# Background work of an attention and FFN kernel in fixed places, one operation at a time

## The chip, the cores and the metric

The kernel runs on one core of a Trainium2 chip. The metric is the time on the device in microseconds (us), lower is better. The core has five engines that run their own instruction queues side by side: PE (TensorE, matrix products; its weight loads are shown apart as PEld), DVE (VectorE), ACT (ScalarE), POOL (GpSimd) and SP (SyncE, which here only issues DMA transfers). Each queue is worked off in order: an instruction that waits holds up everything behind it on its engine.

## What is computed

One transformer block in float32: 16 sequences of 256 tokens, width 256, 16 heads of 128, causal attention, then an FFN with 2048 hidden units whose weights are 4-bit codes with a scale for each 32 values.

```python
def block(x):
    q, k, v = (einsum('bpd,hde->bphe', ln(x), W) + b for W, b in (Q, K, V))
    scores = einsum('bqhe,bkhe->bhqk', q, k) / sqrt(128)
    attn = softmax(where(causal, scores, -1e5))
    z = einsum('bkhe,bhqk->bqhe', v, attn)
    x = x + ln(einsum('bqhe,hed->bqd', z, W_O) + b_O)
    Wg, Wu, Wd = dequant(gate), dequant(up), dequant(down)   # LUT[code] * scale
    h = gelu_tanh(ln(x) @ Wg.T) * (ln(x) @ Wu.T)
    return x + ln(h @ Wd.T)
```

`ln` is a layer norm over the last axis without gain and bias.

## The kernel before

**Tiling.** The 4096 tokens are 8 blocks of 512 (two sequences each). A value that goes into a matrix product is split into a high and a low part (float32r), and three products (high-high, low-high, high-low) make one. In attention a *unit* is one head of one block: `units` lists block b, group g, head j of the group (L375), N = 128 in all; two units are a *pair*, which shares one load of weights. The FFN works on 4 superblocks of 1024 tokens with 8 groups of 256 hidden units each; its gate and up products go by a scheme with seven products in place of eight (class `Two`), for which `x_ops` makes sums and differences of the activations.

**The loop over units** (L941 to L985) is a software pipeline. Iteration i starts the scores and the softmax of unit i+3 (`st_s`), computes K and Q of unit i+4 (`st_qk`), turns the softmax of unit i+3 (`st_t`, a DVE transpose into `tr`), adds to the attention output (`st_o`), multiplies probabilities and values of unit i (`st_z`), splits the probabilities of unit i+1 (`st_p`: `ph` on ACT, `pl` on POOL), computes a part of V (`st_v`), loads the turned probabilities of unit i+2 (`st_b`: `pt` from `hop`) and stores those of unit i+3 (`st_w`: four transfers from `tr` to `hop`). The softmax of a unit goes: `sc` on PE; mask and row minimum `mn` on DVE; exponential `pr` and its sum on ACT; reciprocal `rc` on DVE; scaling of `pr` on POOL; `tr` on DVE; `hop`; `pt`.

**The order is written by hand.** `run` (L98) puts every instruction behind the last one of its engine in program order, and `dma` (L86) does the same for all transfers, which all go out on SP. So the place at which the program issues an operation is its place in its engine's queue.

**Weights.** In the first block, `w_split` splits each weight as it is first used (high part on ACT; low part on DVE for K and Q, on POOL for V and O), and a later `w_keep` writes it back to DRAM. From then on `w_get` (L345) loads the split weights: `wk` and `wq` of pair p+3 at the end of an even iteration, `wo` of pair p+1 and half of `wv` at the end of an odd one (L977), 512 KB each. There are two buffers for each weight.

**Background.** All that isn't the pipeline itself stands in generators, in four queues: `urgent` (`ln1`, the layer norm of the next block's tokens; the FFN's `end`), `splits` (weights of the first block), `behind` (`mid`: attention output back to token order, layer norm, residual, second layer norm, hop into the FFN's order; and `end`) and `idle` (`f_make` for 24 pieces of FFN weights, then `x_ops`). A `yield` ends a step; its number says how many slots to wait, a negative one that the queue goes on to its next step at once if that is due. `slot` (L140) advances a clock, writes what is overdue (`late`), and lets each of the four queues take a step, as long as an account of estimated columns for DVE and POOL (`credit`, `share`, `spent`) isn't overdrawn; `slot(True)` stops after the first. One step can hold several operations on several engines: in `f_make`, three DVE operations in a row (L623 to L625), or four POOL operations, or an ACT copy with a POOL operation behind it (L652).

Slots stand at three places of an iteration: `slot(True)` inside `st_s`, between the first and the second reciprocal and scaling (L463), and two calls behind `st_qk` (L959, L960). The loop over FFN groups has five (L1009 to L1021).

What is needed and not there yet is forced: `await_`, `f_get` (loads of FFN weights) and `Two.product` run steps of a queue until it is there.

Of the kernel before, what the change touches and what calls it, by code (L numbers as in the profile page):

```python
# [28 lines left out]
def kernel(  # L29
# [65 lines left out]

    spent = [0, 0]

    def run(op, dst, *args, **kw):  # L98
        if op.__self__ in (nc.vector, nc.gpsimd):
            cols = max(math.prod(ap.shape[1:]) for ap in (dst, args[0]))  # L100
            if op == nc.vector.tensor_scalar:
                cols //= 2
            spent[op.__self__ is nc.gpsimd] += 100 + cols
        with ExitStack() as behind:
            for m in last.values():
                behind.enter_context(tc.issue_after(m))
            ins = op(dst, *args, **kw)  # L107
        last[ins.ins.engine] = ins.ins
        return ins
# [3 lines left out]
    urgent, behind, splits, idle = deque(), deque(), deque(), deque()  # L113
# [3 lines left out]
    def step(jobs, force=False):  # L117
        while jobs and (force or jobs[0][1] <= now[0]):
            try:
                wait = next(jobs[0][0]) or 1  # L120
            except StopIteration:
                jobs.popleft()
                continue
            jobs[0][1] = now[0] + abs(wait)
            if wait > 0:
                return True
        return False

    def add(jobs, job):
        jobs.append([job, 0])  # L130
# [6 lines left out]
    share = [480, 560]  # L137
    credit = [0, 0]

    def slot(one=False):  # L140
# [3 lines left out]
        for e in range(2):  # L144
            credit[e] = min(credit[e] + share[e], 4 * share[e])
        for jobs in (urgent, splits, behind, idle):
            before = list(spent)
            if (jobs is splits or min(credit) > 0) and step(jobs):
                if jobs is not splits:
                    for e in range(2):  # L150
                        credit[e] -= spent[e] - before[e]
                    if one:
                        return

    def finish(jobs):
        while jobs:
            step(jobs, True)
            overdue(now[0] + 2)

    def await_(found, key, jobs):  # L160
        while key not in found:
            step(jobs, True)
# [6 lines left out]
    def ln_stats(srcs):  # L169
# [5 lines left out]
        for t in range(n):  # L175
            run(nc.vector.bn_stats, st[:, t, :], srcs[t])
            if t % 2:
                yield
        for t in range(n):
            run(nc.vector.bn_aggr, mv[:, t, :], st[:, t, :])  # L180
        run(nc.vector.tensor_scalar, rs[:, :n], mv[:, :n, 1], EPS, None, ALU.add)
        run(nc.gpsimd.tensor_tensor, rs[:, :n], rs[:, :n], mhalf[:, :n], ALU.pow)
        yield
# [5 lines left out]
    def ln_apply(dst, src, mv, rs, t):  # L189
        spent[1] += D  # L190
# [28 lines left out]
    def turn_tokens(hop, xn):  # L219
        tr = wide("xtr").rearrange("p a b -> p (a b)").rearrange("p (k m i) -> p k m i", k=4, m=8)  # L220
        for kt in range(2):
# [5 lines left out]
            yield 1 + kt  # L227
        spread(hop, tr.rearrange("p k m i -> p k (m i)"))
        yield -3

    def split_tokens(key, hop):
        xr = wide("xr")
        dma(xr, hop)
        yield -5
        xr = xr.rearrange("p a (m i) -> p m a i", m=8)
        xt = work.tile([P, 2, 2, TB], F32R, tag="xT", name="xT", bufs=4)
        for kt in range(2):
# [4 lines left out]
            yield  # L242
# [3 lines left out]
    def ln1(b):  # L246
        xs = [x_load(x, b, hf) for hf in range(2)]
        yield -4
        mv, rs = yield from ln_stats([xs[hf][:, t, :] for hf in range(2) for t in range(2)])
        xn = wide("xn")  # L250
        for t in range(4):
            ln_apply(xn[:, t, :], xs[t // 2][:, t % 2, :], mv, rs, t)
            yield
        hop = dram.tile([P, 4, 2 * P], F32, tag="xhop", name="xhop", bufs=2)
        yield from turn_tokens(hop, xn)
        yield from split_tokens((1, b), hop)

    def first_tokens():

        xs = [x_load(x, 0, hf) for hf in range(2)]  # L260
        yield
# [49 lines left out]
    def w_split(p, n):  # L311
# [21 lines left out]
        if done:  # L333
            W[key, n] = w_view(w)
            late.append((now[0] + 2, w_keep, (key, n, w)))
# [5 lines left out]
    def split(p, n):  # L341
        w_split(p, n)
        yield

    def w_get(p, n):  # L345

        if p < NG:
            add(splits, split(p, n))
        elif p < len(pairs):
            overdue(now[0] + 2)  # L350
# [82 lines left out]
    def st_s(u):  # L433
# [22 lines left out]
        for bi in range(2):  # L456
# [5 lines left out]
            if bi:  # L462
                slot(True)  # L463
# [55 lines left out]
    def st_o(p, dh):  # L519
# [13 lines left out]
        if g == NG - 1:  # L533
# [3 lines left out]
            if dh == 1:  # L537
                add(behind, mid(b, PO.pop(b)))
# [11 lines left out]
    def back_load(tr):  # L550
# [3 lines left out]
        yield -3  # L554
        o = wide("o")
        dma(o, hop)
        yield -5
# [8 lines left out]
    def mid(b, oT):  # L566

        tr = back_tile()
        for dh in range(2):
            back(tr, dh, oT[:, dh])  # L570
            yield 1 + dh
        o = yield from back_load(tr)
        xs = [x_load(x, b, hf) for hf in range(2)]
        xt = [xs[t // 2][:, t % 2, :] for t in range(4)]
        mv, rs = yield from ln_stats(o)
        att = wide("att")
        for t in range(4):
            ln_apply(cols4(att[:, t, :]), o[t], mv, rs, t)
            yield
        for hf in range(2):  # L580
            run(nc.gpsimd.tensor_tensor, xs[hf], xs[hf], att[:, 2 * hf : 2 * hf + 2, :], ALU.add)
            yield
# [4 lines left out]
        for t in range(4):  # L587
            ln_apply(pairs_of_h(xn[:, t, :], True), pairs_of_h(xt[t], False), mv, rs, t)
            yield
# [18 lines left out]
    def f_make(g, n, then):  # L608
# [4 lines left out]
        def small_tile(dtype, name):  # L613
            return work.tile([P, 2, 256], dtype, tag="code", name=name, bufs=3)
# [5 lines left out]
        yield  # L620
        if then:
            f_load(*then)
        run(nc.vector.tensor_scalar, sg, c, 8.0, -2.0, ALU.is_ge, ALU.mult)  # L623
        run(nc.vector.tensor_scalar, c, c, 7, None, ALU.bitwise_and)
        run(nc.vector.tensor_scalar, t, c, 2.0, 8.0, ALU.mult, ALU.subtract)  # L625
        yield
        run(nc.vector.scalar_tensor_tensor, v, c, 0.5, t, ALU.mult, ALU.max)
        run(nc.vector.scalar_tensor_tensor, v, c, 2.0, v, ALU.subtract, ALU.max)
        yield
        run(nc.vector.scalar_tensor_tensor, v, sg, 1.0, v, ALU.add, ALU.mult)  # L630
        scb = sc.unsqueeze(1).to_broadcast([P, 2, 256])
        if n == "d":
# [3 lines left out]
            yield  # L636
            run(nc.scalar.copy, w[:, 0], full)
            run(nc.gpsimd.tensor_tensor, w[:, 1], full, f(w[:, 0]), ALU.subtract)
        else:
# [3 lines left out]
            yield  # L643
# [6 lines left out]
            yield  # L650
            w = f_tile("u")
            run(nc.scalar.copy, w[:, 0], full)  # L652
            run(nc.gpsimd.tensor_tensor, w[:, 1, 0:4], full[:, 0:4], f(w[:, 0, 0:4]), ALU.subtract)
            yield
            run(nc.gpsimd.tensor_tensor, w[:, 1, 4:8], full[:, 4:8], f(w[:, 0, 4:8]), ALU.subtract)
        late.append((now[0] + 2, f_keep, (g, n, w)))
        yield
# [12 lines left out]
    def f_get(k, n):  # L670

        sb, g = divmod(k, NG)
        if sb < NSB:
            while (g, n) not in FD:
                step(idle, True)
# [398 lines left out]
```

## Time and profile before

| | |
|---|---|
| Median of 3 runs | 1589.2 us (1588.15 to 1591.8) |
| The profiled execution, its own time | 1585.9 us |
| its span, first to last instruction | 1584.0 us |
| PE busy in the span | 1524.1 us (96%) |
| DVE, ACT, POOL busy | 1182.3, 1021.6, 789.9 us |
| DMA | 407.55 MB, 257 GB/s on average |
| First score matmul of a unit, first and last of the steady part | 74.52 and 1051.27 us |
| First FFN matmul (`pa`) | 1062.63 us |

The span has three stages: attention up to about 1051 us, a passage of some 30 us in which the last units end while the first FFN products run, and the FFN from there, with a tail of 24 us. Times in the profile are counted from the span's first instruction. A busy PE isn't a PE at its peak, since the end of a matmul is modelled and the next one overlaps it: matmuls of 512 columns are shown with 389 ns, and follow each other every 227 ns. So a late start shows as idle time only where it is longer than that overlap, and the distance between the same matmul of two units is the safer measure. In a line of the timeline, what stands in brackets at the end is the idle time of the engine ahead of the instruction and what ended it; `x4` merges four instructions. SPq is SP's queue of DMA issues: the time of such a line is that of the issue, not of the transfer.

### The profile page before, as it was taken

The numbers are of one execution on the slowest core, as the hardware profiler recorded it, in microseconds if no ns is written. First come the engines' busy times: TensorE is split into PE (matmuls) and PEld (weight loads), VectorE is DVE, ScalarE is ACT, GpSimd is POOL, SyncE is SP. The second block draws the span as 40 slices with busy tenths as digits, with TensorE's granted clock in tenths as the row PEclk, the third lists the DMA queues.
The fourth block names the chain that finished last, engine by engine and source line by source line (L and its number), as shares of the span: only waits on it lengthen the run. The fifth ranks groups of instructions, "written<-read, shape, count | busy, mean of one in ns | idle before, by whom it ended". The sixth has DMA issues, their size and how long they took to land.

```text
span 1584.0 us, 25656 instructions
## 1 busy us (share of the span) xinstructions
PE 1524.1 (96%) x7792; PEld 1277.6 (81%) x7792; DVE 1182.3 (75%) x2944; ACT 1021.6 (64%) x2584; POOL 789.9 (50%) x1017
## 2 busy tenths in 40 slices
PE   8999999999899999999999999989999999999996
PEld 6788788888788878878888888877878778778885
DVE  6776777877777777787778787656877777777865
ACT  6786666666666666666666656656565755666663
POOL 3654668668666665765775774670520410420200
PEclk9999999999999999999999999989999999999998
DMA  8897898998889889889898988876566656645551
GB/s 287 286 328 249 271 325 273 314 300 281 283 259 314 282 275 305 265 283 318 259 297 260 303 284 275 275 223 240 194 239 207 232 194 208 237 185 205 222 210 41
DMA packets 200410, 407.55 MB, mean 257 GB/s; under 512 B 21456, under 2 KB 128464, under 8 KB 189520
## 3 DMA queue, kind: packets, MB, share of 16 engines
q1 hardware_dynamic: 200272, 405.91, 77.2%
q8 instruction: 62, 1.02, 0.3%
q14 instruction: 76, 0.62, 0.1%
HBM read 294.15 MB, written 111.67 MB: 256 GB/s over the span
## 4 chain that ended last, share of the span: by engine, by line
PE 46%; DVE 16%; DMA 13%; ACT 10%; POOL 7%; issue 4%; SPq 4%; DVEq 0%; POOLq 0%; ACTq 0%
PE pd L107 10%; PE pa L107 6%; PE pq L107 4%; PE po L107 4%; SPq L91 4%; PE pk L107 4%; PE pf L107 4%; PE pv L107 4%; PE pz L107 4%; PE sc L107 3%; DVE sum L107 3%; DVE tr L107 3%; ACT pr L107 3%; DMA wq<-wq 3%; DMA wk<-wk 2%
## 5 line engine op out<-in xcount | busy, mean ns | idle before, releaser
L107 ACT ACTIVATE pr<-sc,mn 128x128 f32<-128x128 f32 (+1 forms) x512 | 208.3, 420 | 225.8 <-DVE mn L107 209.2
L107 POOL TENSOR_SCALAR pr<-pr,rc 128x128 f32<-128x128 f32 (+1 forms) x512 | 220.0, 444 | 222.2 <-DVE rc L107 211.7
L107 POOL TENSOR_TENSOR rs<-rs,mhalf 128x4 f32<-128x4 f32 (+1 forms) x33 | 35.8, 1084 | 379.6 <-DVE rs L107 374.0
L107 POOL TENSOR_TENSOR pl<-pt,ph 128x512 fp32r<-128x512 f32 x128 | 168.9, 1320 | 94.2 <-ACT ph L107 94.1
L107 PE MATMUL pk<-xT,wk 128*128 128x512 f32 x768 | 200.4, 396 | 12.8 <-DMA wk<-wk 11.1
L107 PE MATMUL pv<-wv,xT 128*128 128x512 f32 x768 | 209.2, 407 | 1.1 <-DVE vl L107 1.1
L107 PE MATMUL pd<-inter,wd 128*128 128x512 f32 x768 | 199.6, 394 | 4.7 <-ACT inter L107 3.1
L107 PE MATMUL pq<-xT,wq 128*128 128x512 f32 x768 | 197.5, 392 | 4.5 <-DMA wq<-wq 3.3
L107 DVE CUSTOM_DVE_ANT_0 sc<-sc,mask 128x128 f32<-128x128 f32 (+1 forms) x512 | 179.9, 372 | 22.2 <-PE sc L107 12.6
L107 PEld LDWEIGHTS pd<-inter,wd 128*128 128x128 f32 x768 | 143.6, 189 | 40.6 <-ACT inter L107 6.4
L107 PEld LDWEIGHTS pq<-xT,wq 128*128 128x128 f32 x768 | 142.8, 188 | 41.2 <-PE pk L107 6.8
L107 PEld LDWEIGHTS pk<-xT,wk 128*128 128x128 f32 x768 | 134.9, 188 | 38.9 <-DMA wk<-wk 14.4
L107 DVE SCALAR_TENSOR_TENSOR kl<-pk,bqk,kh 128x512 fp32r<-128x512 f32 x128 | 95.9, 750 | 93.4 <-ACT kr L107 93.2
L107 ACT COPY part<-pa 128x512 f32<-128x512 f32 x192 | 111.7, 586 | 76.9 <-PE pa L107 74.4
L107 PE MATMUL po<-zh,wo 128*128 128x512 f32 x512 | 158.7, 391 | 0.0
L107 PEld LDWEIGHTS pv<-wv,xT 128*128 128x128 f32 x768 | 135.0, 189 | 25.5 <-DVE vl L107 2.1
L107 ACT CAST inter<-sum 128x512 fp32r<-128x512 f32 x128 | 80.1, 626 | 99.2 <-DVE sum L107 99.0
L107 DVE STREAM_TRANSPOSE tr<-pr 128x768 f32<-128x768 f32 x128 | 123.9, 968 | 15.9 <-POOL pr L107 14.8
L107 DVE TENSOR_TENSOR inter<-sum,inter 128x512 fp32r<-128x512 f32 x128 | 92.5, 723 | 57.8 <-ACT inter L107 55.0
L107 ACT ACTIVATE zh<-pz,bqk 128x512 fp32r<-128x512 f32 x128 | 90.0, 703 | 66.8 <-PE pz L107 66.8
L107 DVE SCALAR_TENSOR_TENSOR zl<-pz,bqk,zh 128x512 fp32r<-128x512 f32 x128 | 92.2, 720 | 49.3 <-ACT zh L107 49.3
L107 PEld LDWEIGHTS po<-zh,wo 128*128 128x128 f32 x512 | 96.5, 189 | 20.2
(139 smaller groups left out, 3807.9 us busy)
## 6 DMA issues: line engine op xcount, KB each, us to landing
hop<-tr SPq DMA_DIRECT2D x512, 96.0 KB, 3.2
pt<-hop SPq DMA_DIRECT2D x128, 384.0 KB, 4.8
wk<-wk SPq DMA_DIRECT2D x64, 512.0 KB, 4.4
wq<-wq SPq DMA_DIRECT2D x64, 512.0 KB, 5.6
wo<-wo SPq DMA_DIRECT2D x64, 512.0 KB, 5.2
wg<-fg SPq DMA_DIRECT2D x32, 1024.0 KB, 5.7
wu<-fu SPq DMA_DIRECT2D x32, 1024.0 KB, 9.6
wv<-wv SPq DMA_DIRECT2D x56, 512.0 KB, 5.5
```

Of the source, the lines that this page charges most:

```text
L91: queue[0] = nc.sync.dma_start(dst, src).ins
L107: ins = op(dst, *args, **kw)
```

## The change

- The account of columns (`spent`, `share`, `credit`) goes. A queue's entry now has a *kind*: the engine that its next step uses, `V_` (DVE), `G_` (POOL), `A_` (ACT, with what POOL adds) or `N_` (transfers only). A `yield` names the kind of the next step and, if not one slot, the slots to wait.
- `slot` gets the kinds that it lets through and, where wanted, a list of queues. It takes **one** step of the first queue whose head is due and of a right kind, and returns; steps of kind `N_` run as well and don't count.
- There are two new queues: `made` (the scaling of a decoded FFN piece, `f_scale`, cut out of `f_make`) and `spare` (`x_ops`). The usual order is splits, urgent, behind, made, spare, idle.
- Steps are cut into single operations: each of `f_make`'s DVE operations but the first two is a step of its own, each layer norm row on POOL is one, and so on. In `f_scale` the cast of 1024 columns is two of 512. The tag `code` has 4 buffers in place of 3.
- An iteration has six places: one for DVE inside `st_s` (splits, idle, urgent, behind), one for DVE ahead of `st_qk`, one for DVE behind it (urgent and behind alone), two for POOL, and one for ACT or POOL at the end. A group of the FFN has five pairs: DVE, then ACT or POOL.
- `wk` and `wq` of pair p+3 are asked for at the head of an even iteration, ahead of `st_s`; `wo` and `wv` stay at the end of an odd one.
- The first FFN weights are asked for in iterations N-9 (`u`) and N-8 (`g`) instead of N-5 (both); `x_ops(0)` is added with the last block's first group instead of its third, and its last operand is made after the loop.
- Waits in slots are rescaled, since there are six in an iteration and not three (`late` by 4 instead of 2, loads by 5 to 8).

```diff
-    def slot(one=False):
+    def slot(kinds, *lanes):
         now[0] += 1
         overdue(now[0])
-        for e in range(2):
-            credit[e] = min(credit[e] + share[e], 4 * share[e])
-        for jobs in (urgent, splits, behind, idle):
-            before = list(spent)
-            if (jobs is splits or min(credit) > 0) and step(jobs):
-                if jobs is not splits:
-                    for e in range(2):
-                        credit[e] -= spent[e] - before[e]
-                    if one:
-                        return
+        for jobs in lanes or (splits, urgent, behind, made, spare, idle):
+            if step(jobs, kinds):
+                return
```

```diff
-    def step(jobs, force=False):
-        while jobs and (force or jobs[0][1] <= now[0]):
+    def step(jobs, kinds=None):
+        while jobs:
+            job, at, kind = jobs[0]
+            if kinds and (at > now[0] or kind not in kinds + N_):
+                return False
             try:
-                wait = next(jobs[0][0]) or 1
+                to = next(job)
+                jobs[0][1:] = (now[0] + to[1], to[0]) if isinstance(to, tuple) else (now[0] + 1, to)
             except StopIteration:
                 jobs.popleft()
-                continue
-            jobs[0][1] = now[0] + abs(wait)
-            if wait > 0:
+            if not kinds or kind != N_:
                 return True
         return False
```

```diff
             if bi:
-                slot(True)
+                slot(V_, splits, idle, urgent, behind)
...
         run(nc.vector.tensor_scalar, sg, c, 8.0, -2.0, ALU.is_ge, ALU.mult)
+        yield V_
         run(nc.vector.tensor_scalar, c, c, 7, None, ALU.bitwise_and)
+        yield V_
         run(nc.vector.tensor_scalar, t, c, 2.0, 8.0, ALU.mult, ALU.subtract)
-        yield
+        yield V_
...
         run(nc.vector.scalar_tensor_tensor, v, sg, 1.0, v, ALU.add, ALU.mult)
+        add(made, f_scale(g, n, v, sc), G_)
+
+    def f_scale(g, n, v, sc):
...
+            w = f_tile("u")
+            yield A_
+            run(nc.scalar.copy, w[:, 0, 0:4], full[:, 0:4])
+            run(nc.gpsimd.tensor_tensor, w[:, 1, 0:4], full[:, 0:4], f(w[:, 0, 0:4]), ALU.subtract)
+            yield G_
             a11, a21, a12, a22, s1, s2, s3, s4 = (full[:, m] for m in range(8))
...
                 run(nc.gpsimd.tensor_tensor, o, l, r, op)
-            yield
-            w = f_tile("u")
-            run(nc.scalar.copy, w[:, 0], full)
-            run(nc.gpsimd.tensor_tensor, w[:, 1, 0:4], full[:, 0:4], f(w[:, 0, 0:4]), ALU.subtract)
-            yield
+            yield A_
+            run(nc.scalar.copy, w[:, 0, 4:8], full[:, 4:8])
             run(nc.gpsimd.tensor_tensor, w[:, 1, 4:8], full[:, 4:8], f(w[:, 0, 4:8]), ALU.subtract)
```

```diff
-            if b == NBLK - 1 and g == 2:
-                add(idle, x_ops(0))
+            if b == NBLK - 1 and g == 0:
+                add(spare, x_ops(0), N_)
+        if not odd:
+            weights((p + 3, "k"), (p + 3, "q"))
         if 0 <= i + 3 < N:
             st_s(i + 3)
+        slot(V_)
         if i + 4 < N:
             st_qk(i + 4)
-        slot()
-        slot()
+        slot(V_, urgent, behind)
+        slot(G_)
+        slot(G_)
...
         if 0 <= i + 3 < N:
             st_w(i + 3)
-        for pn, n in ((p + 1, "o"), (p + 5, "v")) if odd else ((p + 3, "k"), (p + 3, "q")):
-            if pn > {"o": -1, "v": 2}.get(n, 0):
-                w_get(pn, n)
-        if i == N - 5:
-            for n in "gu":
-                f_get(0, n)
+        if odd:
+            weights((p + 1, "o"), (p + 5, "v"))
+        slot(A_ + G_)
+        if N - 9 <= i < N - 7:
+            f_get(0, "ug"[i - (N - 9)])
```

## The prediction

> **What bounds the kernel now.** I read the page's first two parts, then the stretches by stage, then PE's waits, then short timelines around those waits.
>
> ```profile
> span 1584.0 us, 25656 instructions
> PE 1524.1 (96%) x7792; PEld 1277.6 (81%) x7792; DVE 1182.3 (75%) x2944; ACT 1021.6 (64%) x2584; POOL 789.9 (50%) x1017
> ...
> 74.50:1051.30 976.80, 949.45 (x5237) 811.94 (x5238) 750.03 (x2147) 652.19 (x1857) 643.52 (x867) 1.00 0.88 284
> 1051.30:1081.00 29.70, 24.15 (x111) 19.44 (x110) 10.56 (x24) 14.78 (x29) 10.62 (x12) 0.83 0.79 278
> 1081.00:1560.00 479.00, 474.51 (x2065) 385.10 (x2063) 359.97 (x597) 297.73 (x548) 94.97 (x75) 1.00 0.57 207
> ```
>
> The stretches are attention without its start, the passage to the FFN, and the FFN. After the stretch and its length stand the busy times of PE, PEld, DVE, ACT and POOL, then granted clock, DMA share and GB/s. PE sets the time, so only time that PE loses can be won. An undisturbed attention unit takes 7.83 us: the first score matmuls stand at 1035.60, 1043.44 and 1051.27 in the timeline. The first stretch holds 119 units, from 74.52 to 1051.27; 119 x 7.83 = 931.8, so **45.0 us are lost there** (27.4 us of it shows as idle PE, the rest as matmuls that start late behind a modelled end). The passage loses 29.70 - 24.15 = 5.6 us idle, and 0.17 x 29.70 = 5.0 us by its lower clock: **10.6 us**. The FFN loses 4.5 us. Start and tail are left as they are.
>
> ```profile
> PE pk L107 <- DMA wk<-wk: 11.1, 10, 2.4
> PE sc L107 <- ACT qr L107: 10.3, 18, 1.4
> PE pz L107 <- POOL pl L107: 5.0, 8, 1.5
> PE pq L107 <- DMA wq<-wq: 3.3, 6, 0.8
> ...
> ACT wu L107 <- POOL full L107: 25.4, 11, 3.9
> ```
>
> These are waits: us in total, times, longest. PE waits most for K's and Q's weights (14.4 us), then for work that ACT, DVE and POOL finish late.
>
> ```profile
> 1013.50 0.43 SPq L91 DMA_DIRECT2D wk<-wk  x1
> 1013.98 0.58 SPq L91 DMA_DIRECT2D wq<-wq  x1
> ...
> 1020.88 1.56 PE L107 MATMUL pk<-xT,wk 128*128 128x512 f32 x6
> 1021.97 0.44 SPq L91 DMA_DIRECT2D wo<-wo  x1
> ...
> 947.90 0.51 DVE L107 TENSOR_SCALAR sg<-codes 128x512 bf16<-128x512 int32 x1
> 948.44 1.40 DVE L107 TENSOR_SCALAR codes<-codes 128x512 int32<-128x512 int32 x1
> 949.87 0.43 DVE L107 TENSOR_SCALAR t<-codes 128x512 bf16<-128x512 int32 x1
> 950.22 0.97 DVE L107 STREAM_TRANSPOSE tr<-pr 128x768 f32<-128x768 f32 x1
> ...
> 952.64 0.37 ACT L107 ACTIVATE pr<-sc,mn 128x128 f32<-128x128 f32 x1 [4.13 <-DVE mn L107]
> ```
>
> The weights of the pair whose first unit computes `pk` at 1020.88 are issued at 1013.50: a lead of 7.4 us, against 4.4 us (K) and 5.6 us (Q) median to landing. Any hold-up on SP of 2 to 3 us reaches PE, as at 422.23, where the issue came 4.66 us ahead of `pk` at 426.89 and PE sat idle 2.40 us. The second group shows a burst: five decoding operations stand on DVE from 947.38 (two `codes`, `sg`, `codes`, `t`) ahead of `tr`; then `zl` and the masks come late, ACT idles 4.13 us for `mn`, and at 956.09 PE starts `sc` 0.97 us late for `qr`.
>
> **A. K's and Q's loads at the head of an even unit.** Before, they are issued at the end of unit i, behind `st_b` and the four `hop` issues of that unit; after, ahead of these, directly behind `wo` and `wv` of unit i-1. The buffer they fill (two per weight) belonged to the pair used last in unit i-1, whose `pq` is over before that unit's `po`, for which `wo` waits anyway, so no new wait on PE comes in. The issue of `wo` stands 2.25 us into its following unit (1021.97, the unit starting at 1019.72); with `wv` (0.4) and `wk` (0.4) before it, `wq` goes out about 3.2 us into unit i and is needed some 1.2 us into unit i+2 (1020.88 - 1019.72): 15.66 + 1.2 - 3.2 = 13.7 us of lead. Against that stand 5.6 us to landing plus `wo` and `wv` ahead of it: 1 MB at the highest rate of a 40 us stretch, 335 GB/s, is 3.1 us. 5.0 us stay in hand, so the 14.4 us go. What is moved past: two issues of 0.4 us each on SP, ahead of `pt` and `hop` of unit i. `pt` waits for its buffer until about 6.7 us into a unit (1018.56 against 1011.89), so SP has the time. Bounds: 10 (some waits stay) to 18 (late starts without an idle row go too).
>
> **B. One operation in each place, by engine.** Before, three calls of `slot` in a unit each run up to four steps, and a step holds up to three DVE operations, four POOL operations or an ACT copy that waits for POOL. After, six places take at most one step each: DVE between the reciprocals, DVE behind them, DVE behind `ql` (only `urgent` and `behind`), POOL twice behind `pr`, and ACT or POOL at the end. Each place is priced against the idle time there in quiet units:
> - First DVE place: rc waits 0.64 us for ACT (1015.39); an operation takes 0.41 to 0.80 us by the page's means: up to 0.16 us exposed, where the step with `sg`, `codes` and `t` now holds the second rc from 427.38 to 428.85.
> - Second: `kl` waits 0.78 us for `kr` (1016.34): covered.
> - Third: `ql` ends at 1017.55 and `tr` waits for POOL until 1019.17; without a POOL operation between the `pr` pairs that wait shrinks, and `tr` is late by 0.7 us at most instead of 2.8. If that cover goes, `hop` and `pt` are late next; `pt` has 8.4 us (1010.73 to 1019.12) against 4.8 to landing.
> - POOL: `pl` 1.3 and `pr` 1.7 us plus three operations of 1.3 are 6.9 of 7.83 us.
> - ACT: the copy takes 0.63 us where ACT idles 0.97 us for `mn` (1013.65); the 1.05 us cast of `wu` is cut in halves, and its POOL operands are a place older, so the 25.4 us of ACT's waits mostly go.
>
> The operations are the same, so nothing is saved in busy time. Of the 45.0 us, A takes 14.4; of the other 30.6 I let a third stay (DMA contention, the weight splits, which last until 110 us, chains that are late by themselves) and take **20**. Bounds: 0 (the bursts weren't the cause) to 28.
>
> Does the work still fit? A piece needs 7 DVE places, 24 pieces need 168; `idle` comes second in the first place, in 114 units, and gets the second place when `urgent` and `behind` have no DVE step. These need 15 in 16 units and have three places, so some 8 of 16 are left: 114 + 56 = 170. It just fits, as now (the last `fd` store is at 963).
>
> **C. The passage.**
>
> ```profile
> 1059.62 0.39 PE L107 MATMUL pz<-pl,vh 128*128 128x256 f32 x1 [1.49 <-POOL pl L107]
> ...
> 1062.63 1.65 PE L107 MATMUL pa<-xT,wg 128*128 128x512 f32 x3 [1.46 <-DMA wg<-fg]
> 1065.60 1.65 PE L107 MATMUL pa<-xT,wu 128*128 128x512 f32 x3 [1.32 <-DMA wu<-fu]
> ```
>
> `wu` and `wg` are now asked for in units 119 and 120 instead of 123, and the FFN's operands start 4 units earlier in a lane of their own. That takes away 1.46 + 1.32 us, and the 1.28 and 1.27 us of POOL (`wk`, `wq`) that stood ahead of `pl` at 1055.84, so the 1.49 us too. The last unit's chain (`sc` 1051.27, then `pr`, `tr`, `hop`, `pt`, `pl`) still has little PE work to lie under. The clock share of 0.83 came with gaps of 1.49 us and less. I take **5** of the 10.6 us; bounds 0 and 10. The 2 MB of `wu` and `wg` add 128 GB/s to 284 in two units, over the 346 GB/s seen at 1056 to 1063: up to 3 us late there, inside the bounds.
>
> The Trainium skill, "TensorE: Matmul & The Clock Gate", section "What's actually happening", has the clock halve after at least one idle window of about 3.4 us. This trace shows half speed with no single gap that long. By the page the clock would stay up once the two DMA gaps are gone, and C would be near 10; by the row it may still fall.
>
> **D. FFN.** Five pairs of places instead of five calls; 4.5 us can be won and ACT and POOL are half idle: 0, bounds -5 to 3.
>
> **The sum.** 14 + 20 + 5 = 39. The profiled execution took 1585.9 us (span 1584.0 and 1.9 around it): 1546.9. The median of the runs shown, 1589.2, is 3.3 us above it, so I forecast **1550 us**; its own bounds, A to D not all at one end, 1536 to 1563.
>
> **The rivals.**
> - *Only the loads count.* Late `qr` and `pl` stay because DVE and POOL have the same work in the same unit. For it: DVE is busy 750 of 976.8 us. Against it: ACT's longest waits stand behind stacked operations. A plus 3 of C: 1589.2 - 17 = 1572. Chance 0.2.
> - *The loads crowd out the softmax's hops: slower.* `wo`, `wv`, `wk`, `wq` now go out together: 2 MB, 6.3 us at 335 GB/s. If `pt` still lay behind all of it, it would land at 4.8 + 6.3 = 11.1 us against 8.4 in hand: 2.7 us late on ACT, less the 1.1 us by which `pl` is early (1016.3 to 1017.4): 1.6 us in each of 56 pairs, 90 us: 1550 + 90 = 1640. It decides from 4.7 us of queue ahead of `pt` on, and is dearer than all gains from 5.4 us on. Against it: `pt` goes out some 3.5 us after `wk`. Chance 0.07.
> - *Too few places: slower.* If the second place never comes free, 54 DVE steps, 8 pieces, are left for the FFN, forced in one go where a group asks for them: 4.8 us on DVE, 5.6 on POOL, some 10 us a piece exposed: 80 us, 1630 where all is exposed, 1590 to 1595 where half is. Against it: the count above. Chance 0.06.
> - *It doesn't do what it says:* the waits only change their names, since DMA is at 0.88. Against it: 976.8 us at 284 GB/s are 277 MB, 828 us at 335. 1586 to 1592. Chance 0.05.
>
> On the second rival, the Trainium skill, "DMA: Bandwidth & Descriptors", section "Queues, rings and completion order", says that an engine consumes descriptors in ring order, all of SP's on one row. By that the whole burst does stand ahead of `pt`; the landing of `pt` in the changed trace decides, and none here shows four such loads in a row.
>
> **How the numbers follow.** My forecast has 0.62. The range 1533 to 1580 holds most of it and of the first rival. Within 0.2% (3.2 us) is about what a measurement of this kernel can tell from no change. Faster: 0.62 + 0.2 = 0.82; same 0.05; slower 0.07 + 0.06 = 0.13.
>
> **What would show it.** A: `wk` issued 13 us or more ahead of its `pk`, and no DMA among PE's waits for `pk` and `pq`. B: never more than one background operation between rc and `kl`, or between `ql` and `tr`; ACT's waits for `mn` and PE's for `qr` clearly down; attention units near 7.83 us. C: `pa` without a DMA wait; a clock near 1.00 in the passage. I am wrong if `pt` lands after ACT asks for it, if `wu` and `wd` are still made in the FFN, or if units stay near 8.2 us without a DMA wait.

## The result, and the profile after

The changed kernel takes **1565.6 us** in the median of four runs (1558.9 to 1566.3), beside 1588.8 for the kernel before on the same chip: a ratio of 0.984 (95% interval 0.981 to 0.987), 23 us gained where 39 were forecast. That lies in the forecast's range of 1533 to 1580, and above the 1536 to 1563 that the bounds of its terms gave. The profiled execution is the quickest of the four, 1558.9 us, so what is read from it below belongs to a time some 7 us under the median.

Of the changed kernel, first the page's span and PE line, then the stretches attention without its start, passage, and FFN, with the columns as in the prediction:

```profile
span 1556.9 us, 25639 instructions
PE 1514.1 (97%) x7792; PEld 1278.6 (82%) x7792; DVE 1180.7 (76%) x2944; ACT 1028.6 (66%) x2600; POOL 807.1 (52%) x1017
...
74.50:1030.00 955.50, 939.97 (x5224) 810.88 (x5223) 745.14 (x2142) 655.49 (x1867) 657.73 (x861) 1.00 0.88 292
1030.00:1060.00 30.00, 26.47 (x140) 21.60 (x139) 14.95 (x30) 19.45 (x37) 16.92 (x17) 1.00 0.78 250
1060.00:1535.00 475.00, 471.41 (x2054) 383.26 (x2053) 361.39 (x596) 295.78 (x544) 89.87 (x75) 1.00 0.55 207
```

The same matmuls, DVE and POOL work as before stand in a shorter span. The 119 units from 74.9 to 1032.5 take 957.6 us: 25.8 us over 119 x 7.83, against 45.0 before, so attention gave 19.2 us. The passage now loses 3.5 us idle at full clock, against 10.6 us: 7 us. The FFN loses 3.6 us, against 4.5.

Now the waits of the changed kernel (us in total, times, longest), PE's first, then the largest that changed on ACT:

```profile
PE pz L99 <- POOL pl L99: 9.2, 12, 0.9
PE sc L99 <- ACT qr L99: 4.9, 11, 1.0
...
PE pk L99 <- DMA wk<-wk: 1.7, 1, 1.7
...
ACT ph L99 <- DMA pt<-hop: 112.1, 49, 6.6
...
ACT pr L99 <- DVE mn L99: 68.2, 87, 3.9
```

The same two rows of ACT in the kernel before:

```profile
ACT pr L107 <- DVE mn L107: 209.2, 116, 5.8
...
ACT ph L107 <- DMA pt<-hop: 10.6, 6, 6.0
```

Two of the forecast signs are there: PE's wait for K's and Q's weights is down from 14.4 us to 1.7, and ACT's wait for `mn` from 209.2 to 68.2. One sign of a wrong forecast is there too: `pt` lands after ACT asks for it 49 times (112.1 us), against 6 times (10.6 us) before, and what PE still waits for in attention is named mostly `pl` (9.2 us), `qr` (4.9) and `ph` (3.2), the work behind `pt`. Nearly all of the loss lies in a few units. Most distances from unit to unit are 7.83 us; those behind units 41, 43, 57, 73, 75, 85, 89, 101, 105 and 117 are 8.4 to 11.9, and hold 21.1 of the 25.8 us. (One more, behind unit 18, is 9.8.) At each of the ten ACT had waited 4.5 us or more for the `pt` of the unit three before; the 39 other waits, up to 3.5 us, cost PE next to nothing. The ten come about in two ways.

Behind units 41, 57, 73, 89 and 105 `pt` is issued late. SP's issues before the last of them:

```profile
839.94 0.34 SPq L91 DMA_DIRECT2D pt<-hop  x1
...
842.34 0.43 SPq L91 DMA_DIRECT2D wo<-wo  x1
842.81 0.43 SPq L91 DMA_DIRECT2D wv<-wv  x1
843.28 2.76 SPq L91 DMA_DIRECT2D ohop<-oback  x4
846.09 0.50 SPq L91 DMA_DIRECT2D wk<-wk  x1
846.63 0.64 SPq L91 DMA_DIRECT2D wq<-wq  x1
847.72 2.56 SPq L91 DMA_DIRECT2D xhop<-xtr  x4
850.41 1.39 SPq L91 DMA_DIRECT2D o<-ohop  x1
851.84 1.48 SPq L91 DMA_DIRECT2D xs<-in_x  x2
854.27 0.34 SPq L91 DMA_DIRECT2D pt<-hop  x1
```

From `wo` to `xs` SP spends 10.2 us on issuing alone (the sum of the second column), more than a whole unit, and the next `pt` goes out 14.3 us after the last one instead of 7.8. Steps of kind `N_` run in every place and don't count, so up to six places of a unit can put transfers on SP; here the last block's output goes back to token order (`ohop`, `o`) and the next block's tokens are loaded, with `wk` and `wq` among them. The price, on ACT and on PE:

```profile
859.23 0.62 ACT L99 CAST ph<-pt 128x512 fp32r<-128x512 f32 x1 [6.62 <-DMA pt<-hop]
...
859.89 0.39 PE L99 MATMUL pz<-ph,vh 128*128 128x256 f32 x1 [1.35 <-ACT ph L99]
```

ACT idles 6.62 us for `pt`, and PE starts `pz` late. The landing isn't slow here: `ph` starts 4.96 us after the issue of `pt`, where the forecast took 4.8; it is the issue that is late.

Behind units 43, 75, 85, 101 and 117 it is mostly the landing. There `pt` goes out 6.2 to 10.2 us after the last one, but behind the four loads of weights and the store of a decoded piece of the FFN. Before the first of them, with `wo` and `wv` just ahead:

```profile
344.75 0.39 SPq L91 DMA_DIRECT2D fu<-wu  x1
345.77 0.32 SPq L91 DMA_DIRECT2D wk<-wk  x1
346.14 1.03 SPq L91 DMA_DIRECT2D wq<-wq  x1
347.33 0.56 SPq L91 DMA_DIRECT2D pt<-hop  x1
...
358.37 0.62 ACT L99 CAST ph<-pt 128x512 fp32r<-128x512 f32 x1 [5.81 <-DMA pt<-hop]
```

This `pt` was issued 6.2 us after the last one, and `ph` could start only 11.0 us later; at the other four, `ph` starts 8.3 to 9.7 us after the issue. It is the usual case, too: 42 of the 49 waits, 107.5 of the 112.1 us, are in even units, whose `pt` from the second block on follows `wo`, `wv`, `wk` and `wq`, and there `ph` starts 8.0 us after the issue of `pt` in the median.

The Trainium skill, "DMA: Bandwidth & Descriptors", section "Queues, rings and completion order", has each DMA engine consume descriptors in ring order, by which the 2 MB of loads delay the landing of a `pt` right behind them. The trace agrees: a `pt` 1.2 us behind `wq` took 11.0 us, and the one that goes out 7.6 us after `wq` 4.96.

### The profile page after: what moved, and what is told of

Same layout as the page of the kernel before. It is cut to its first block, busy times and chain, and to the rows that moved or that the text cites. A ratio compares the mean times of both kernels' runs of the same rounds, so it can differ in the third digit from the quotient of the medians.

```text
span 1556.9 us, 25639 instructions
## 1 busy us (share of the span) xinstructions
PE 1514.1 (97%) x7792; PEld 1278.6 (82%) x7792; DVE 1180.7 (76%) x2944; ACT 1028.6 (66%) x2600; POOL 807.1 (52%) x1017
## 4 chain that ended last, share of the span: by engine, by line
PE 72%; DMA 11%; DVE 6%; ACT 5%; SPq 3%; issue 2%; POOL 1%; DVEq 0%; POOLq 0%; ACTq 0%
PE pd L99 11%; PE pk L99 9%; PE pv L99 8%; PE pq L99 8%; PE po L99 8%; PE sc L99 7%; PE pz L99 7%; PE pa L99 7%; PE pf L99 5%; DMA pt<-hop 4%; SPq L91 3%; DVE sum L99 3%; PE pe L99 2%; DMA hop<-tr 2%; DMA wq<-wq 1%
## 5 line engine op out<-in xcount | busy, mean ns | idle before, releaser
L99 POOL TENSOR_TENSOR pl<-pt,ph 128x512 fp32r<-128x512 f32 x128 | 165.0, 1289 | 246.2 <-ACT ph L99 234.9
L99 POOL TENSOR_SCALAR pr<-pr,rc 128x128 f32<-128x128 f32 (+1 forms) x512 | 248.6, 501 | 65.5 <-DVE rc L99 65.4
L99 ACT ACTIVATE pr<-sc,mn 128x128 f32<-128x128 f32 (+1 forms) x512 | 208.9, 422 | 74.4 <-DVE mn L99 68.2
L99 ACT CAST ph<-pt 128x512 fp32r<-128x512 f32 x128 | 79.4, 620 | 113.0 <-DMA pt<-hop 112.1
L99 ACT CAST inter<-sum 128x512 fp32r<-128x512 f32 x128 | 80.1, 626 | 101.1 <-DVE sum L99 101.0
```

## The experiments

Three questions were open: what the early loads are worth, what the late `pt` costs, and which part of "one operation, by engine, in six places" made the gain. The table has the median, the ratio to the kernel before in the same session with its interval, the loss of units 8 to 127 against 7.83 us each in the profiled execution, and two waits.

| Kernel | us | ratio | units lose | PE for `wk` | ACT for `pt` |
|---|---|---|---|---|---|
| before | 1588.8 | | 45.0 | 11.1 | 10.6 |
| changed | 1565.6 | 0.984 (0.981 to 0.987) | 25.8 | 1.7 | 112.1 |
| changed, again | 1566.7 | 0.985 (0.983 to 0.988) | 29.0 | 2.5 | 114.8 |
| 1 loads back at the end | 1563.5 | 0.984 (0.982 to 0.986) | 34.5 | 22.9 | 16.7 |
| 2 before, with early loads | 1600.8 | 1.008 (1.006 to 1.011) | 56.0 | 0.5 | 60.6 |
| 3 `pt` ahead of the loads | 1582.3 | 0.996 (0.994 to 0.997) | 49.4 | 32.9 | 43.3 |
| 4 transfers last | 1575.1 | 0.992 (0.990 to 0.993) | 25.5 | 0.6 | 101.1 |
| 5 transfers last, steady part | 1563.1 | 0.985 (0.983 to 0.988) | 21.0 | 1.3 | 136.7 |
| 6 as 5, loads at the end | 1553.9 | 0.979 (0.977 to 0.981) | 8.2 | 4.2 | 8.5 |
| 7 passage as before | 1567.4 | 0.987 (0.985 to 0.989) | 28.9 | 1.0 | 114.7 |
| 9 as 6, third DVE place for all | 1545.7 | 0.973 (0.972 to 0.975) | 16.7 | 9.3 | 6.0 |
| 10 as 6, decoding in bursts | 1546.8 | 0.973 (0.971 to 0.975) | 20.3 | 13.0 | 9.6 |
| 11 as 9, every queue in a place | 1579.8 | 0.994 (0.992 to 0.995) | 36.2 | 10.0 | 4.4 |
| 12 as 9, any engine in a place | 1638.8 | 1.030 (1.029 to 1.032) | 95.7 | 33.4 | 6.9 |

**1. The loads back at the end of the even unit, all else as changed.**

```diff
-        if not odd:
-            weights((p + 3, "k"), (p + 3, "q"))
         if 0 <= i + 3 < N:
             st_s(i + 3)
...
-        if odd:
-            weights((p + 1, "o"), (p + 5, "v"))
+        weights(*(((p + 1, "o"), (p + 5, "v")) if odd else ((p + 3, "k"), (p + 3, "q"))))
```

> The changed kernel with K's and Q's loads back at the end of an even unit, behind pt and hop; all else stays. Theory (the loads' place is worth what PE waited for them, 14 us, but costs a part of it again because pt now queues behind them): PE's waits for wk and wq come back, 8 to 15 us; ACT's wait for pt falls from 112 us to under 50; the time is 3 to 10 us above the changed kernel's 1565.6, 1569 to 1576. Rival (the loads' place is the whole gain): 1585 or more. Rival (the loads' place does nothing once the background is spread): within 3 us of 1565.6 and no wait for wk.

The waits went as expected and the time didn't: 1563.5 us. PE waits 22.9 us for `wk` again and no longer for `pl` and `ph`; ACT's wait for `pt` falls from 112.1 to 16.7. So the move exchanges one wait for another of about the same cost. The two profiled executions favour the early loads (1558.9 against 1564.9), the medians the late ones by 2 us, and the intervals are the same: in this kernel the move is worth nothing that can be measured. All of the 25 us that this kernel gains belong to the rest of the change.

**2. The early loads alone, in the kernel before.**

```diff
+        if not odd and p + 3 > 0:
+            for n in "kq":
+                w_get(p + 3, n)
         if 0 <= i + 3 < N:
             st_s(i + 3)
```

The same two `w_get` leave the end of the even unit.

> The kernel before with nothing but K's and Q's loads moved to the head of an even unit. Theory: PE's waits for wk and wq (11.1 + 3.3 us) go, bursts of background stay, PE's wait for qr stays near 10 us; some pt comes late: 1589 - 14 + 4 = 1579, 1574 to 1584. Rival (the lateness on SP is caused by the bursts themselves, so the loads stay late): within 3 us of 1589.

It came out on the other side, 12 us **slower**. PE's waits in this kernel:

```profile
PE sc L107 <- ACT qr L107: 18.0, 27, 1.4
PE pz L107 <- POOL pl L107: 16.6, 18, 2.8
```

The wait for `wk` is gone (0.5 us), but `qr` costs 18.0 instead of 10.3 and `pl` 16.6 instead of 5.0. ACT waits 60.6 us for `pt` instead of 10.6, and `ph`, `pl` and all that stands behind `ph` on ACT, `qr` too, come late with it. This profiled execution is 14.2 us longer than the one before the change: the units lose 11 us more, and the first block ends 4.5 us later (unit 8 starts at 79.0, not 74.5).

**3. `pt` first, then the loads, then `hop`.**

```diff
         if 0 <= i + 2 < N:
             st_b(i + 2)
+        if not odd:
+            weights((p + 3, "k"), (p + 3, "q"))
         if 0 <= i + 3 < N:
             st_w(i + 3)
```

> The changed kernel with K's and Q's loads between the load of pt and the stores to hop, in even units. Theory (pt is late because it stands behind wk and wq on SP): ACT's wait for pt falls from 112 us to 60 or less, the loads keep about 9 us of lead, so few waits for wk: 1559 to 1563 in the median. Rival (what holds pt is the background's transfers, ohop, xhop, o and xs, not the loads): ACT's wait for pt stays over 90 us, time within 2 us of 1565.6. Rival (the rate of the DMA engines, not the order, holds pt): wait unchanged and wk late too, 1566 to 1575.

1582.3 us. Behind `pt` the loads wait with it: `pt` waits until the `hop` it reads has landed, and SP now idles 277.3 us for that (223.8 in the changed kernel), with `wk` and `wq` behind it. PE waits for `wk` 10 times, up to 5.5 us. ACT's wait for `pt` fell as expected, to 43.3 us, and the time rose all the same: of the three places tried in the changed kernel, the one directly behind an issue that waits is the worst.

**4 and 5. Transfers last.** Steps of kind `N_` may run only in the last place of a unit, behind all of the unit's own transfers; in 5 only in iterations 16 to 111.

```diff
-            if kinds and (at > now[0] or kind not in kinds + N_):
+            if kinds and (at > now[0] or kind not in kinds):
...
-        slot(A_ + G_)
+        slot(A_ + G_ + N_)
```

In 5 the first line reads `kinds + (N_ if anywhere[0] else "")`, and `anywhere[0] = not 16 <= i < N - 16` is set at the head of an iteration. In both, the last place of each of the FFN's five pairs takes `N_` too.

> The changed kernel with steps that only transfer (kind N_) let through in the last place of a unit alone, behind pt and hop; before, any place could run them, so that ohop, xhop, o and xs of a block's start stood ahead of pt. Theory: the long waits for pt (6.6 us at 859.2, 5.2 us at 340.1) go, ACT's wait for pt falls from 112 us to 70 or less, attention loses 8 to 12 us less: 1553 to 1560 in the median. Rival (wk and wq, not these, hold pt): within 2 us of 1565.6. Rival (the rate of the DMA engines holds it): within 2 us, with the same long waits elsewhere.

> The changed kernel with steps that only transfer let through in the last place of a unit alone, but only in units 16 to 111; in the first block, in the last one and in the FFN any place runs them as in the changed kernel. Theory (the cluster ohop, xhop, o and xs ahead of pt makes the stalls at the block starts): the steady units lose under 3 us against 7.83 us a unit where the changed kernel loses some 25, and the clock falls less: 1540 to 1550. Rival (the stalls only moved into the places where transfers_last lost time): 1560 to 1570.

Both theories missed their times; the rival of 5 named its 1563.1 us. In 4 the steady blocks are quiet (from unit 16 to 112 they lose 3.6 us, where the changed kernel loses 23.0), but the first block's end isn't: `ln1` of block 1 comes so late that PE stands still for 16.3 us in one unit, and the passage waits 6.4 us for `wg`. In 5 the units lose 21.0 us instead of 25.8 to 29.0, and the passage gives it back, 6.0 us for `wg` and 1.9 for `wu`. ACT's wait for `pt` doesn't shrink at all (136.7 us), so the background's transfers alone don't make `pt` late; the early loads do. Yet 4 has them too, with 101.1 us of ACT's wait, in steady blocks that lose next to nothing: the wait has to pass what the pipeline can spare before PE feels it. Why the same rule leaves 15.4 us in units 16 to 112 of 5 isn't shown.

**6. As 5, with the loads at the end of the even unit** (the two edits of 1 and 5).

> The kernel transfers_last_steady with K's and Q's loads back at the end of an even unit. Theory (with the cluster out of the way the loads' place matters little, since SP is no longer held up for more than the 7 us of lead): within 4 us of transfers_last_steady, with PE's waits for wk under 5 us. Rival (the early loads are needed for themselves): 8 to 14 us slower than it, with waits for wk of 8 us and more.

1553.9 us, 9 better than 5 with intervals that don't touch. ACT's wait for `pt` is 8.5 us and PE's for `wk` only 4.2: with the background's transfers out of the way, the old place of the loads is good enough, and the new one costs 9 us. Beside 1, which differs only in the place of the transfers, it is 9.6 us better. What is left is the passage, one PE row, and a stretch around it with its clock in the column behind POOL:

```profile
1066.83 1.62 PE L99 MATMUL pa<-xT,wg 128*128 128x512 f32 x3 [6.04 <-DMA wg<-fg]
...
1062.80:1076.50 13.70, 7.64 (x17) 5.62 (x18) 3.77 (x7) 2.84 (x5) 0.00 (x0) 0.50 0.87 322
```

SP issues `wg` only at 1061.20, behind `wd` at 1060.82, and the last `fd` store of the decoded pieces is at 1062.15, against 963.2 in the kernel before: the pieces have run out of places.

**7. The passage's own edits taken back.**

```diff
-            if b == NBLK - 1 and g == 0:
+            if b == NBLK - 1 and g == 2:
...
-        if N - 9 <= i < N - 7:
-            f_get(0, "ug"[i - (N - 9)])
+        if i == N - 5:
+            for n in "gu":
+                f_get(0, n)
```

> The changed kernel with the first FFN weights asked for in unit N-5 again, both at once, and x_ops(0) added at the third group of the last block as before; all else stays. Theory (these two are the passage's gain): PE waits for wg and wu again (1.5 and 1.3 us) and the passage from 1030 to 1060 us loses 3 to 8 us more, its clock below 1.00: 1569 to 1574. Rival (the quiet attention units alone let the last chain end in time): within 2 us of 1565.6.

1567.4 us, within 2 us of the changed kernel's two medians. PE waits 1.6 us for `wu`. By the medians the earlier requests for `wu` and `wg` and the earlier `x_ops` are worth 2 us at most. The traces say more: from the first score matmul of the last unit to the end of the span it takes 529.4 us here, 524.4 and 523.6 in the two traces of the changed kernel and 532.7 before, while the units lose as much as in the second of the two (28.9 and 29.0). But those two are of executions quicker than their medians. So whether these edits are worth 2 us or 5 stays open.

**8. The changed kernel again**, to see what its spread is.

> The changed kernel as it is, once more, beside the others: its profile was taken from a run of 1558.9 us, and three others took 1565.5 to 1566.3 us at a lower mean clock (0.989 to 0.991 against 0.994). Theory (after some of the stalls at block starts PE runs at half speed for 3.4 or 6.8 us, in some runs oftener): the median is near 1565, and a profile at the lower clock shows more of these stretches, at block starts. Rival (the difference lies in the passage to the FFN): the stretch at half speed stands near 1030 to 1060 us.

1558.97 to 1567.95 us, at mean clocks of 0.995 and 0.989: the spread goes with the clock (below), though not alone, since 1562.28 and 1566.66 us both came at 0.990.

**9. The third DVE place open to the pieces.** As 6, with:

```diff
-        slot(V_, urgent, behind)
+        slot(V_, urgent, behind, idle)
```

> The kernel transfers_last_loads_at_end with the third DVE place of a unit open to the decoding of FFN weights (idle) too. In transfers_last_loads_at_end the last of the 24 pieces was stored at 1062 us, so that a load of wd held SP until 1060.8 and PE waited 6.0 and 2.0 us for wg and wu, with 13.7 us at half speed. Theory (the pieces end too late, because the places just suffice): the last fd store comes before 1010 us, these waits go, attention stays within 10 us of 7.83 us a unit: 1536 to 1544. Rival (three DVE operations in most units crowd tr and kl): attention loses 10 us more, 1550 or over.

**1545.7 us**, 20 better than the changed kernel and 43 better than the one before, the best of all, and 1.7 us above what the theory allowed. The last `fd` store is at 822.6 instead of 1062.2, and the passage has neither a DMA wait nor a lower clock; that is worth more than the 8.5 us by which the units of this profiled execution lose more than those of 6. PE waits 1.9 us for `qr`; ACT's wait for `mn`:

```profile
ACT pr L99 <- DVE mn L99: 86.2, 124, 3.4
```

**10. Decoding in bursts of two and three DVE operations.** As 6, three `yield V_` of `f_make` taken out, and 6 buffers of `code`:

```diff
         run(nc.vector.tensor_scalar, sg, c, 8.0, -2.0, ALU.is_ge, ALU.mult)
-        yield V_
         run(nc.vector.tensor_scalar, c, c, 7, None, ALU.bitwise_and)
-        yield V_
         run(nc.vector.tensor_scalar, t, c, 2.0, 8.0, ALU.mult, ALU.subtract)
         yield V_
```

The third is behind the first `scalar_tensor_tensor`.

> The kernel transfers_last_loads_at_end with f_make's three tensor_scalar operations in one step again and its first two scalar_tensor_tensor in one, as before the change; the tag code has 6 buffers. Theory (operations one at a time are what quieted attention): PE waits for qr and zl again, attention loses 6 to 15 us more against 7.83 us a unit than the 7 us of transfers_last_loads_at_end; the pieces end earlier, so the passage is better by some 10 us: 1550 to 1558 in all. Rival (what counted was the order of the transfers, and bursts are hidden): attention loses no more than there, 1540 to 1545.

1546.8 us, between the two ranges. The units do lose 12.1 us more than those of 6, as the theory had it, but not by its waits: PE waits for `qr` 1.9 us, as in 6 and 9, and most of the loss is the wait for `wk` (13.0 us). Since a piece needs fewer places, the pieces end at 738.6, and the passage is clean as in 9. Against 9, which decodes in single operations and also ends its pieces early, bursts cost 1 us in the median, within the spread. The theory that single DVE operations quieted attention falls for the decoding.

**11 and 12. What a place lets through.** As 9, but in 11 each place lets every queue take a step of a right kind, and in 12 each place takes one step of any engine.

```diff
         for jobs in lanes or (splits, urgent, behind, made, spare, idle):
-            if step(jobs, kinds):
-                return
+            step(jobs, kinds)
```

```diff
-            if step(jobs, kinds):
+            if step(jobs, kinds and V_ + G_ + A_ + (N_ if N_ in kinds else "")):
                 return
```

> The kernel third_place_for_all, but a place lets every queue take a step of the right engine instead of one queue alone, so that two or three operations can stand in one place, as before the change. Theory (one operation in a place is what quieted attention): PE waits for qr, pl and zl again and the units lose 5 to 15 us more: 1552 to 1562. Rival (as bursts_of_decoding already hints, operations of the right engine are hidden even when stacked; what counts is the place): within 4 us of 1545.7.

> The kernel third_place_for_all, but a place lets through a step of any engine, still one step: POOL and ACT work can stand between the reciprocals and ahead of pl or kh again. Theory (the engine named by the place is what counts): ACT's waits for POOL and PE's for pl and qr return, 8 to 20 us more: 1554 to 1566. Rival (only the number of operations in a place counts): within 4 us of 1545.7.

Both signs were right and both sizes too small: 34 us for several queues, of which some 20 lie in the units and the rest behind the last of them, and **93 us** for the engine, 79 of them in the units. Of the waits that were named, `pl` returns in 11 (6.6 us) and `qr` in 12, with 33.4 us for `wk`, the largest there. With any engine in any place units 24 to 79 lose 9 to 13 us in every eight, until the decoding is nearly done. Waits of kernel 12, PE's, then ACT's:

```profile
PE sc L99 <- ACT qr L99: 31.6, 28, 3.0
...
ACT pr L99 <- DVE mn L99: 220.5, 120, 5.3
```

ACT's wait for `mn` is back at 220.5 us (209.2 before the change, 86.2 in 9). One reservation: with more steps in a unit the decoding can also run faster. In 12 it doesn't run faster than in 10 (first and last `fd` store at 228.3 and 739.9 us, 216.8 and 738.6 in 10), whose units lose 20.3 us and not 95.7, so its pace isn't what makes 12 slow. In 11 it does (last store at 622.3), and there place and pace aren't told apart.

## Why the prediction was right on the sign and wrong on the size

**A, the loads (14.4 us forecast, 0 to -2 measured): the step that failed.** Its first half held: the loads are issued earlier, `wk` some 11 us ahead of its `pk` in the median of the pairs (some 6 before, both from the starts in the timelines), though not the 13.7 forecast, and the wait is all but gone. The half that failed is "What is moved past: two issues of 0.4 us each on SP, ahead of `pt` and `hop` of unit i", "so SP has the time". It counts the issues, and not the bytes that then stand ahead of `pt`: in an even unit four loads, 2 MB, where before the change two stood ahead of each `pt`. So where ACT waits for the `pt` of an even unit, it comes 8.0 us after its issue in the median, not 4.8, and up to 11.0. Nor does SP have the time in those units in which a block's own transfers go out: at 842.34 to 853.32 the loads stand in a row of 10.2 us of issuing. And `pt` doesn't catch up at once. The next `hop` goes out behind it and must land before the following `pt` (854.27, then 860.31: 6.04 us), so only some 1.8 us of a lag are made good in a unit. The 14.4 us for `wk` came back as late `ph` and `pl`. The move alone costs the kernel before 12 us (2), is worth nothing in the changed kernel (1), and costs 9 us where the background's transfers stand last (5 against 6), though the steady units of 4 show that it needn't.

**B, the places (20 forecast): right in size, for another reason.** With the loads at the end, places and passage together give 25 us (1); 20 + 5 were forecast. The sign named for it is there, ACT's wait for `mn` at a third. But the cause was given as the bursts of `f_make`, and 10 shows that bursts of two or three DVE operations in a DVE place cost nothing that can be measured. What counts is that the place names its engine and takes one queue (for the second, place and pace aren't told apart): undoing the first costs 93 us, the second 34 (12 and 11 against 9). The step missed that `N_` steps run uncounted in every place.

**"It just fits, as now".** The count of 170 places for 168 steps was right as a warning and wrong as an "as now": the last `fd` store went from 963.2 to 1042.0 in the changed kernel, to 1062.2 in 6. One more place was worth 8 us (9 against 6). The rival of too few places named the mechanism; here it was worth some 8 us and not 40 to 80, since only the last pieces were late.

**C, the passage (5 forecast, 7 seen).** The size was right; whether for the cause that was named is open, since the edits made for it are worth 2 us at most by the medians and some 5 by the traces (7).

**D** (0 forecast) came to 0.9 us.

**The sum**: 25 of B and C with A at 0 to -2 make the 23 measured, instead of 39. **The rivals**: *only the loads count* is the reverse of what was found. *The loads crowd out the softmax's hops* is what happened, with its mechanism and its sign of a late `pt`. Its 11.1 us to landing is the worst case of the trace (11.0, the median 8.0), and its 2.7 us late on ACT the mean of 42 even units (2.6). What it had wrong is the price. It let 1.1 us pass before PE is late, and left out that `pl` itself stood 3.1 us behind the end of `ph` in the unit that it was read from (1011.89 and 1015.03); in the changed trace waits up to 3.5 us cost PE next to nothing. So there are ten stalls and 21 us, not 56 and 90 us, and five of the ten come by issue time and not by bytes; alone, in 2, the move does make the kernel slower. *The waits only change their names* is true of A alone.

## What to carry to other kernels

Before moving a prefetch to an earlier place in an in-order queue, add up the issue time in the busiest unit, not in a usual one, and the bytes that then stand ahead of what is needed within one unit. When background work is put between the steps of a pipeline, give each place an engine that idles there and let one queue through: that was worth 93 and 34 us here (for the second the pace may have a part), while cutting the decoding's DVE steps finer was worth nothing and can use up the places; the other cuts weren't tried alone. Transfers need a place too, even if they cost no engine: it was worth 9.6 us with the loads at the end (6 against 1).

## What the hardware did that was not expected

**The clock.** In the changed kernel the clock halves right behind the stall of unit 105 shown above. Two stretches of it, clock behind POOL:

```profile
858.50:862.10 3.60, 1.40 (x10) 1.16 (x10) 1.10 (x3) 2.88 (x10) 2.18 (x2) 1.00 0.67 212
862.10:865.50 3.40, 3.40 (x12) 2.82 (x12) 3.40 (x10) 3.40 (x9) 3.32 (x8) 0.50 0.92 277
```

PE was busy 1.40 of the 3.60 us before, with no gap over 1.35 us, and then ran at half speed for 3.4 us with all its work at hand. In the second profiled execution of the same kernel this came four times, 3.4 us each (at 600.5, 733.6, 962.3 and 1044.2, the first three in units that stall, the last in the passage), with PE busy 1.1 to 1.7 of the 3.4 us before, and not behind unit 105. From unit 73 to 74 it took 9.68 us in the one, without it, and 12.12 in the other, with it. So a stall of some 2 us may cost 2 more, by chance. That is of the size of the spread from 1559 to 1568 us; the slowest of these executions have no trace. Kernel 6 had 13.7 us at half speed, from 1062.8 on, within its gap of 6.04 us.

The Trainium skill, "TensorE: Matmul & The Clock Gate", section "What's actually happening", has a free-running window of about 3.4 us. The stretches agree with it in length (3.4 us, and four times that in 6), in their starts (in the second execution 133.1, 228.7 and 81.9 us apart, 39, 67 and 24 times 3.41), and in their coming in one execution and not in the other. Its "idle window" needn't be wholly idle: 1.40 of 3.60 us were busy here.
